# A two-layer graph network in fp32: one of seven products done in seven quarter products, and the output added in DRAM

## The chip, the cores and the metric

The kernel runs on one core of a Trainium2 chip. The time is device microseconds, the median of several runs; three runs of the kernel before gave 2488.0, 2488.44 and 2492.84 us. A profile of one more execution (2488.91 us) shows where the time lies. In tables PE is TensorE's matmuls, PEld its weight loads, DVE VectorE, ACT ScalarE, POOL GpSimd and SP SyncE.

## What is computed

128 graphs of 128 nodes with 512 features share one adjacency matrix. Two layers follow one another, each on a layer norm with a relu:

```python
# layer 0
h = relu(layernorm(x))
q, k, v = h @ Wq.T, h @ Wk.T, h @ Wv.T
rel = adj.T * (q @ k.T)
rel = rel / norm(rel, axis=2)
x = x + rel @ v
# layer 1
h = relu(layernorm(x))
q, k, v = h @ Wq + bq, h @ Wk + bk, h @ Wv + bv      # 8 heads of 64
scores = q @ k.T / 8 + where(adj == 0, -1e9, 0)
x = x + softmax(scores) @ v
```

All of it is fp32, inputs and output are x of 128x128x512.

## The kernel before

**Groups.** Four graphs make a group; there are 32 groups. In layer 0 the weights of Q and K are multiplied with each other once, so that layer 0 has two large products for each group (G and V) and layer 1 three (Q, K, V). Each is a product of 512x512 activations with 512x512 weights.

**Seven products for eight.** `Product` does each by the Winograd form of Strassen's method: both operands are cut into 2x2 quarters of 256x256, and seven products of quarters (`P1` to `P7`) and a few sums of quarters replace the eight. Each is four matmuls with a 128x128 stationary operand and a 128x256 moving one (`mm`, line 229). Sums of the weights' quarters are made once (`sums`), those of h for each group on VectorE (`sumA`, `sumB`). P1 and P2 together make the first quarter of the result: P1's result is kept in SBUF (`keep`), and VectorE adds P2's, out of PSUM, to it (`add`, line 253). For Q and K a bias is added on ScalarE while a result is kept (line 240); for layer 1's V it is on VectorE (line 246).

**Transposes by way of DRAM.** h, the softmax weights and the attention output are transposed by a store to scratch DRAM (`send_blocks`, on ScalarE's queue), a load back in blocks of 32 (`fetch_blocks`, on SyncE's queue, into two buffers `u` in turn), and a transpose of 32x32 blocks on VectorE: `hn`, `rd`, `T` for h; `ex`, `wr`, `wt` for the softmax weights; `oc`, `rdo`, `ot` for the output.

**The order.** All engines' queues follow one list of steps written by hand. Each engine takes its own instructions in the list's order. `FIRST`, `SECOND` and `LAST` are for the ends, `ORDER` runs for 30 of the 32 periods. In a period `m` is layer 0 of one group, `l` layer 1 of the group before it, `p` the end of the one before that, `f` the loading and statistics of the next, and `n` is `m`'s own layer 1 coming up. TensorE's part of `ORDER`, from the middle on, is layer 1's V (V.P1, P2, P5, P6, P3, P7), the scores `S3`, the first half of the attention `A0`, V.P4, and then with the next period Q.P1, Q.P2, K.P1, K.P2, Q.P5, Q.P6, Q.P3 and so on.

**The names that matter here.** `stat` makes a graph's mean and variance on VectorE, `inv` turns them into scale and shift on GpSimd, `hn` applies them on ScalarE. `mk3` masks the scores of graph 3, `exC2` and `exD2` are the two halves of graph 2's exponentials, `wr2` and `wt2` bring its transposed weights. `ot` (line 643) ends a pair of graphs: VectorE transposes (line 649) and scales by the softmax sums (line 654), GpSimd adds the result to x in SBUF (line 661) and stores it (line 662). x stays in one of 12 buffers from its load to that store.

**PSUM.** Eight banks: four in turn for products (`mm`), two for one graph's scores, two in turn (`po`) for `R`, `O`, `A` and half-score tiles.

Of the kernel before, what the change touches and what calls it, by code (L numbers as in the profile page):

```python
# [21 lines left out]
def kernel(  # L22
# [15 lines left out]
    nc = tc.nc  # L38
# [6 lines left out]
    HF = D // 2  # L45
    PSUM = bass.MemoryType.PSUM

    const = ctx.enter_context(tc.tile_pool(name="const", bufs=1))
    xpool = ctx.enter_context(tc.tile_pool(name="xpool", bufs=12))
    hpool = ctx.enter_context(tc.tile_pool(name="hpool", bufs=1))  # L50
    ppool = ctx.enter_context(tc.tile_pool(name="ppool", bufs=1))
    rpool = ctx.enter_context(tc.tile_pool(name="rpool", bufs=4))
# [42 lines left out]
    raw = {}
    for name, w, tag in (("q", wq0, "pq"), ("k", wk0, "pk"), ("v", wv0, "pv0")):
# [20 lines left out]
    def weights0(between):  # L117

        a12 = rpool.tile([P, 2, HF], F32, tag="r", name="a12")

        idle = ps_o.tile([P, P], F32, tag="po", name="idle")
        for _ in range(16):
            nc.tensor.transpose(idle, ident, ident)
        pa = [ps_mm.tile([P, D], F32, tag="mm", name=f"pa_{m}") for m in range(KD)]
        for k in range(KD):
            for m in range(KD):
                nc.tensor.matmul(
                    pa[m], lhsT=raw["q"][:, k, ts(m, P)], rhs=raw["k"][:, k, :],
                    start=(k == 0), stop=(k == KD - 1),
                )  # L130
# [30 lines left out]
    class Weights1:  # L161
# [7 lines left out]
        def sumw(self):  # L169
            sums("v0", w12["v0"], nc.gpsimd)  # L170

        def loadx(self):
            for b in range(G):
                load(2, b, nc.gpsimd)

        def sumq(self):
            sums("q", w12["q"], nc.vector)

# [27 lines left out]
    class Product:  # L206
# [65 lines left out]

        def P4(self):
            self.copy(self.quarter(1, 0), self.mm("x", T4N, self.h.x22, False), 0)

    class Layer:
        n: int
# [92 lines left out]
        def sumB(self):  # L370
            nc.vector.tensor_tensor(self.s[3], self.x12, self.s[1], ALU.subtract)
            nc.vector.tensor_tensor(self.s[2], self.x11, self.x21, ALU.subtract)

        def turned(self, k, b):
            return self.half[b // 2][:, k, ts(b % 2, P)]

    class Layer0(Layer):
        n = 0

        def start(self):  # L380
            g = self.g
            self.gT = ppool.tile([P, KD, G * P], F32, tag="pgv", name=f"gT_{g}")
            self.v = ppool.tile([P, G, D], F32, tag="pv0", name=f"v0_{g}")
            self.po = {}
            self.G = Product(self, "a", self.gT, True, name=f"pg_{g}")
            self.V = Product(self, "v0", self.v, False, name=f"pv0_{g}")
# [54 lines left out]
    class Layer1(Layer):  # L441
        n = 1

        def start(self):
            g = self.g
            self.qT = ppool.tile([P, NH, G * P], F32, tag="pq", name=f"qT_{g}")
            self.kT = ppool.tile([P, NH, G * P], F32, tag="pk", name=f"kT_{g}")
            self.Q = Product(self, "q", self.qT, True, bq_sb, name=f"pq_{g}")
            self.K = Product(self, "k", self.kT, True, bk_sb, name=f"pk_{g}")
            self.rs, self.wT, self.ps, self.nmax, self.po, self.e = {}, {}, {}, {}, {}, {}  # L450
            self.half_s = {}
            self.dw, self.uw, self.total, self.do, self.uo = {}, {}, {}, {}, {}
# [190 lines left out]
        def ot(self, i):  # L643
            g, u = self.g, self.uo.pop(i)
            for n in range(2):
                b = 2 * i + n
                xb = x_tiles.pop((g, b))
                o = work.tile([P, NH, TB, BK], F32, tag="o", name=f"o_{g}_{b}")
                nc.vector.transpose(
                    o.rearrange("p k t q -> p t k q"),  # L650
                    u[:, n * TB : (n + 1) * TB].rearrange("p t (k q) -> p t k q", q=BK),
                )
                heads = o.rearrange("p k t q -> p k (t q)").rearrange("p k (r d) -> p k r d", r=2)
                nc.vector.tensor_tensor(  # L654
                    heads, heads,
                    self.rs.pop(b).rearrange("p (r k) -> p k r", r=2)[:, :, :, None].to_broadcast(
                        [P, NH, 2, HD]
                    ),
                    ALU.mult,
                )  # L660
                nc.gpsimd.tensor_tensor(xb, xb, o.rearrange("p k t q -> p (k t q)"), ALU.add)  # L661
                nc.gpsimd.dma_start(out[g * G + b], xb)

    FIRST = """
        m.sumA m.sumB m.start f.stat0 f.stat1 f.inv0 m.G.P1 m.G.P2 f.stat2 f.stat3 f.inv1 w.sumw m.G.P5 f.hn0 f.rd0 m.G.P6
        w.scale m.G.P3 m.V.P1 f.hn1 f.rd1 w.sumv w.loadx m.G.P7 m.V.P2 w.sumq m.G.P4 m.V.P5
        m.R m.mask_rel m.square f.T0 m.V.P6 m.V.P3 m.N m.norms m.V.P7 m.O0 m.xO0 m.O1 m.xO1 n.stat0 n.stat1  # L670
        n.inv0 m.V.P4 n.hn0 n.rd0 f.T1 f.start f.G.P1 f.sumA m.O2 m.xO2 m.O3 m.xO3 n.stat2 n.stat3 n.inv1
        f.G.P5 f.sumB f.G.P6 n.hn1 n.rd1 f.G.P3 f.G.P7 n.T0 f.G.P2 f.G.P4 w.sumk n.T1 n.start
    """.split()
    SECOND = """
        l.Q.P1 l.sumA l.Q.P2 l.sumB l.K.P1 l.K.P2 l.Q.P5 l.Q.P6 f.load0 f.load1 l.Q.P3 l.K.P5 l.K.P6 l.Q.P7
        l.K.P3 l.K.P7 l.S0 l.mk0 f.load2 f.load3 l.Q.P4 l.K.P4 l.ex0 l.wr0 m.V.P1 f.stat0 f.stat1 f.inv0
        m.V.P2 m.V.P5 m.R m.mask_rel m.square f.stat2 f.stat3 f.inv1 m.V.P6 l.S1 m.N l.S2 l.mkA1 m.norms l.exC1
        l.mkB1 l.exD1 l.wr1 l.wt0 m.V.P3 l.add_mask2 m.V.P7 m.O0 m.xO0 m.O1 m.xO1 n.stat0 n.stat1 n.inv0
        m.V.P4 l.mx2 n.hn0 n.rd0 l.exC2 l.exD2 l.wr2 l.start_v l.V.P1 m.O2 m.xO2 m.O3 m.xO3 n.stat2 n.stat3 n.inv1
        l.V.P2 l.wt1 l.V.P5 n.hn1 n.rd1 l.V.P6  # L680
        l.V.P3 n.T0 l.V.P7 l.S3 l.A0 l.mk3 l.oc0 l.wt2 l.V.P4 l.ex3 n.T1 n.start
    """.split()
    ORDER = """
        l.Q.P1 p.rdo0 l.sumA l.Q.P2 p.wr3 m.hn0 l.sumB l.K.P1 m.rd0 l.K.P2 p.ot0 l.Q.P5 l.Q.P6 m.hn1 m.rd1
        l.Q.P3 l.Q.P7 p.wt3 m.T0 l.K.P5 l.K.P6 l.Q.P4 f.load0 f.load1 l.K.P3
        l.K.P7 m.T1 m.sumA m.sumB m.start m.G.P1 l.K.P4 m.G.P2 l.S0 p.A1 l.mk0 p.oc1 p.rdo1 m.G.P5 m.G.P6
        l.ex0 l.wr0 m.G.P3 m.V.P1 m.G.P7 p.ot1 m.V.P2 f.stat0 f.stat1 f.inv0 m.G.P4 m.V.P5
        l.wt0 f.load2 f.load3 m.R m.mask_rel m.square m.V.P6 l.S1 m.N l.S2 l.mkA1 m.norms l.exC1 l.mkB1 l.exD1
        l.wr1 m.V.P3 l.add_mask2 m.V.P7 m.O0 m.xO0 m.O1 m.xO1 n.stat0 n.stat1 n.inv0 m.V.P4 l.mx2
        n.hn0 n.rd0 l.exC2 l.exD2 l.wr2 l.start_v l.V.P1 m.O2 m.xO2 m.O3 m.xO3 n.stat2 n.stat3 n.inv1  # L690
        l.V.P2 l.wt1 l.V.P5 n.hn1 n.rd1 l.V.P6 f.stat2 f.stat3 f.inv1
        l.V.P3 n.T0 l.V.P7 l.S3 l.A0 l.mk3 l.oc0 l.wt2 l.V.P4 l.ex3 n.T1 n.start
    """.split()
# [21 lines left out]
    with tc.manual_schedule(engines={EN.PE, EN.SP, EN.Pool, EN.DVE, EN.Activation}):  # L715
        p, l, m = None, None, Layer0(0)
# [9 lines left out]
        f = Layer0(1)  # L726
# [40 lines left out]
```

## Time and profile before

| What | Value |
|---|---|
| median of three runs | 2488.44 us (2488.0 to 2492.84) |
| profiled execution | 2488.91 us, span 2487.1 us |
| TensorE busy, granted clock | 2479.4 us (100%), 1.000 |
| VectorE, ScalarE, GpSimd busy | 1724.2 us (69%), 1027.0 us (41%), 531.0 us (21%) |
| one period of `ORDER` | 76.55 us |
| data moved by DMA | 405.72 MB, mean 163 GB/s |
| x loads and output stores | 124 DMAs of 256 KB each on GpSimd's queue, median 3.1 and 3.0 us from issue to landing |

The profile gives for each engine its busy time, and for groups of equal instructions the mean time of one. The chain of waits follows the work back from the last instruction, at each step to what released it. A timeline lists one engine's instructions with start, length, and in brackets the idle time before and what ended it.

### The profile page before, as it was taken

The numbers are of one execution on the slowest core, as the hardware profiler recorded it, in microseconds if no ns is written. First come the engines' busy times: TensorE is split into PE (matmuls) and PEld (weight loads), VectorE is DVE, ScalarE is ACT, GpSimd is POOL, SyncE is SP. The second block draws the span as 40 slices with busy tenths as digits, with TensorE's granted clock in tenths as the row PEclk, the third lists the DMA queues.
The fourth block names the chain that finished last, engine by engine and source line by source line (L and its number), as shares of the span: only waits on it lengthen the run. The fifth ranks groups of instructions, "written<-read, shape, count | busy, mean of one in ns | idle before, by whom it ended". The sixth has DMA issues, their size and how long they took to land.

```text
span 2487.1 us, 40880 instructions
## 1 busy us (share of the span) xinstructions
PE 2479.4 (100%) x14688; PEld 2114.3 (85%) x14688; DVE 1724.2 (69%) x2549; ACT 1027.0 (41%) x3248; POOL 531.0 (21%) x944
## 2 busy tenths in 40 slices
PE   9999999999999999999999999999999999999999
PEld 7888888888888888888888888888888888888888
DVE  5666776667766677766677666776667776667766
ACT  3344443444433444434444344443344443343434
POOL 5111222122212212122122211221211212212111
PEclk9999999999999999999999999999999999999999
DMA  6256554565644556445555455554455644555544
GB/s 202 81 164 178 178 163 150 156 180 166 186 145 147 179 169 193 145 146 168 178 178 162 150 155 182 166 180 148 147 174 173 189 144 145 176 175 181 153 131 141
DMA packets 370619, 405.72 MB, mean 163 GB/s; under 512 B 29616, under 2 KB 287024, under 8 KB 370416
## 3 DMA queue, kind: packets, MB, share of 16 engines
q1 hardware_dynamic: 279520, 168.71, 26.4%
q10 hardware_dynamic: 70000, 165.96, 18.4%
q0 software_dynamic: 20896, 68.44, 8.4%
q8 instruction: 116, 1.90, 0.3%
q14 instruction: 87, 0.71, 0.1%
HBM read 204.80 MB, written 198.18 MB: 162 GB/s over the span
## 4 chain that ended last, share of the span: by engine, by line
PE 94%; DMA 2%; DVE 2%; issue 1%; SPq 1%; ACT 0%; POOL 0%; ACTq 0%; DVEq 0%; POOLq 0%
PE pv_x L229 16%; PE pg_x L229 9%; PE pq_x L229 8%; PE pk_x L229 8%; PE pv_z L229 8%; PE pg_z L229 5%; PE pr L393 5%; PE pq_z L229 5%; PE po L626 4%; PE pk_z L229 4%; PE pv_y L229 4%; PE po L433 4%; PE pss L471 4%; PE pg_y L229 2%; PE pq_y L229 2%; PE pk_y L229 2%
## 5 line engine op out<-in xcount | busy, mean ns | idle before, releaser
L661 POOL TENSOR_TENSOR xb<-xb,o 128x512 f32<-128x512 f32 x124 | 158.0, 1274 | 1175.2 <-DVE o L654 1157.4
L229 PE MATMUL pv_x<-wc_v,h 128*128 128x256 f32 x1280 | 300.8, 382 | 0.7 <-DVE pv_r L246 0.7
L229 PEld LDWEIGHTS pv_x<-wc_v,h 128*128 128x128 f32 x1280 | 240.4, 190 | 51.6 <-issue 20.0
L229 PE MATMUL pv_z<-wc_v,s 128*128 128x256 f32 x1024 | 245.1, 382 | 0.0
L324 DVE STREAM_TRANSPOSE h<-u_h 128x1024 f32<-128x1024 f32 x126 | 156.5, 1242 | 113.6 <-DMA u_h<-d_h 112.0
L312 ACT ACTIVATE hn<-xb,shift,rstd 128x512 f32<-128x512 f32 x252 | 191.0, 807 | 74.4 <-POOL shift L304 57.2
L229 PEld LDWEIGHTS pv_z<-wc_v,s 128*128 128x128 f32 x1024 | 191.9, 190 | 28.7
L495 ACT ACTIVATE e<-pss,nmax 128x128 f32<-128x128 f32 x504 | 177.7, 384 | 38.9 <-DVE nmax L488 38.9
L229 PE MATMUL pv_x<-wc_v,s 128*128 128x256 f32 x768 | 181.7, 379 | 0.0
L229 PE MATMUL pq_x<-h,wc_q 128*128 128x256 f32 x768 | 181.5, 379 | 0.0
L229 PE MATMUL pk_x<-h,wc_k 128*128 128x256 f32 x768 | 181.5, 379 | 0.0
L637 ACT COPY oT<-po 128x512 f32<-128x512 f32 x124 | 72.7, 586 | 259.6 <-PE po L626 196.2
L294 DVE BATCH_NORM_STATS2 st<-xb 128x6 f32<-128x512 f32 x256 | 171.9, 672 | 8.7 <-DMA xb<-in_x_dram 8.7
L229 PEld LDWEIGHTS pq_x<-h,wc_q 128*128 128x128 f32 x768 | 145.8, 190 | 19.9
L229 PEld LDWEIGHTS pk_x<-h,wc_k 128*128 128x128 f32 x768 | 145.8, 190 | 19.9
L510 DVE STREAM_TRANSPOSE wT<-u_w 128x1024 f32<-128x1024 f32 x126 | 152.8, 1213 | 9.4 <-DMA u_w<-d_w 8.1
L229 PEld LDWEIGHTS pv_x<-wc_v,s 128*128 128x128 f32 x768 | 143.3, 190 | 18.4 <-issue 0.2
L301 POOL TENSOR_SCALAR rstd<-mv 128x2 f32<-128x2 f32 x128 | 28.4, 222 | 478.1 <-DVE mv L295 475.7
L654 DVE TENSOR_TENSOR o<-o,rs 128x512 f32<-128x512 f32 x124 | 124.3, 1003 | 4.3
L229 PE MATMUL pg_z<-s,wc_a 128*128 128x256 f32 x512 | 124.1, 385 | 0.0
L229 PE MATMUL pq_z<-s,wc_q 128*128 128x256 f32 x512 | 121.8, 381 | 1.4 <-DVE qT L253 1.2
L626 PE MATMUL po<-wT,v 128*64 128x128 f32 x1984 | 122.0, 276 | 0.0
(157 smaller groups left out, 4839.0 us busy)
## 6 DMA issues: line engine op xcount, KB each, us to landing
d_h<-hn ACTq DMA_DIRECT2D x126, 512.0 KB, 4.2
u_h<-d_h SPq DMA_DIRECT2D x504, 128.0 KB, 3.8
d_w<-e ACTq DMA_DIRECT2D x126, 512.0 KB, 3.0
u_w<-d_w SPq DMA_DIRECT2D x504, 128.0 KB, 3.3
xb<-in_x_dram POOLq DMA_DIRECT2D x124, 256.0 KB, 3.1
d_o<-oT ACTq DMA_DIRECT2D x62, 512.0 KB, 3.7
u_o<-d_o SPq DMA_DIRECT2D x248, 128.0 KB, 3.2
out_dram<-xb POOLq DMA_DIRECT2D x124, 256.0 KB, 3.0
```

The costliest lines, as they stand in the source:

```text
L229: nc.tensor.matmul(ps[:, m, :], lhsT=lhsT, rhs=rhs, start=first and m == 0 and k == 0, stop=k == 1, skip_group_check=True,)
L294: nc.vector.bn_stats(st, x_tiles[g, b])
L312: nc.scalar.activation(hn[:, r], x_tiles[g, b].rearrange("p (k j q) -> p j k q", j=TB, q=BK), AF.Relu, bias=self.shift[:, b : b + 1], scal ...
L324: nc.vector.transpose(half.rearrange("p k (t i) -> p t k i", i=BK), self.u.pop(i).rearrange("p t (k q) -> p t k q", q=BK),)
L393: nc.tensor.matmul(pr[:, b, :], lhsT=self.turned(k, b), rhs=self.gT[:, k, ts(b, P)], start=(k == 0), stop=(k == KD - 1),)
L433: nc.tensor.matmul(po, lhsT=self.rel[:, b, :], rhs=self.v[:, b, :], start=True, stop=True)
L471: nc.tensor.matmul(half[r][:, k, :], lhsT=self.qT[rows, k, ts(b, P)], rhs=self.kT[rows, k, ts(b, P)], start=True, stop=True,)
L495: nc.scalar.activation(e[:, :, i, :], sc[:, i, :].rearrange("p (j q) -> p j q", q=BK), AF.Exp, bias=nmax[:, i : i + 1], accum_out=self.tot ...
L510: nc.vector.transpose(self.wT[b].rearrange("p h (t i) -> p t h i", i=BK), self.uw.pop(b).rearrange("p t (h q) -> p t h q", q=BK),)
L626: nc.tensor.matmul(po[r * HD : (r + 1) * HD, k, :], lhsT=self.v[:, b, ts(2 * k + r, HD)], rhs=wT[:, r * NH + k, :], start=True, stop=True,)
L654: nc.vector.tensor_tensor(heads, heads, self.rs.pop(b).rearrange("p (r k) -> p k r", r=2)[:, :, :, None].to_broadcast([P, NH, 2, HD]), ALU ...
L661: nc.gpsimd.tensor_tensor(xb, xb, o.rearrange("p k t q -> p (k t q)"), ALU.add)
```

## The change

P2 of Q and of layer 1's V is done, in the periods that run `ORDER`, by the same method once more: its operands are cut into 2x2 pieces of 128x128, and seven products of pieces, each one matmul of 128x128x128, replace the eight that four 128x256 matmuls hold. All seven go into one PSUM bank, `i`, in four slots that are used again; what the method adds up in a slot stays there and is accumulated. Between them results leave the slots by ScalarE copies and VectorE adds. The first quarter's missing addend, P1's result, is added at the end by GpSimd. The sums of pieces of the weights are made once on GpSimd (`sums2`), those of h for each group, also on GpSimd (`sumX`).

Layer 1's x is stored to the output in DRAM on SyncE's queue (`sto`) once its layer norm has read it; later the attention output is added to it there by a DMA that accumulates, on GpSimd's queue. GpSimd's add in SBUF goes away, and x has 8 buffers for 12. The loads of the third group move from the first period to the second. In the list the two halves of graph 2's exponentials move behind V.P2a and V.P2b, `wr2` with them, the statistics `f.stat2` and `f.stat3` behind V.P2c, and in `LAST` V.P6 moves ahead of graph 2's maxima.

```diff
-    xpool = ctx.enter_context(tc.tile_pool(name="xpool", bufs=12))
+    xpool = ctx.enter_context(tc.tile_pool(name="xpool", bufs=8))
...
+    def sums2(n: str, eng):
+        w, t = wc[n][:, W21], wi[n]
+        w11, w12_, w21, w22 = w[:, 0, 0:P], w[:, 0, P:HF], w[:, 1, 0:P], w[:, 1, P:HF]
+        eng.tensor_tensor(t[:, 0], w12_, w11, ALU.subtract)
+        eng.tensor_tensor(t[:, 1], w22, t[:, 0], ALU.subtract)
+        eng.tensor_tensor(t[:, 2], w22, w12_, ALU.subtract)
+        eng.tensor_tensor(t[:, 3], w21, t[:, 1], ALU.subtract)
...
-        def loadx(self):
-            for b in range(G):
-                load(2, b, nc.gpsimd)
...
+        def mi(self, slot: int, w, x, first=False):
+            if first:
+                pool, tag = (ps_o, "po") if self.turned else (ps_mm, "mm")
+                self.ps["i"] = pool.tile([P, 4, P], F32, tag=tag, name=f"{self.name}_i")
+            lhsT, rhs = (w, x) if self.turned else (x, w)
+            nc.tensor.matmul(
+                self.ps["i"][:, slot, :], lhsT=lhsT, rhs=rhs, start=first, stop=True, skip_group_check=True
+            )
...
+        def plus(self, i, j, slot):
+            nc.vector.tensor_tensor(self.block(i, j), self.ps["i"][:, slot, :], self.block(i, j), ALU.add)
+
+        def P2a(self):
+            self.mi(0, self.wq(0, 0), self.xq(0, 0), True)
+            self.mi(1, self.wq(1, 0), self.xq(0, 1))
+            self.mi(2, self.i[:, 0], self.h.sx[:, 0])
+            nc.scalar.copy(self.block(0, 0), self.ps["i"][:, 0, :])
+            nc.scalar.copy(self.block(1, 1), self.ps["i"][:, 2, :])
+
+        def P2e(self):
+            self.plus(0, 0, 1)
+
+        def P2b(self):
+            self.mi(0, self.i[:, 1], self.h.sx[:, 1])
+            self.mi(2, self.wq(1, 1), self.h.sx[:, 3])
+            nc.scalar.copy(self.block(0, 1), self.ps["i"][:, 0, :])
+
+        def P2f(self):
+            self.plus(0, 1, 2)
+
+        def P2c(self):
+            self.mi(0, self.i[:, 2], self.h.sx[:, 2])
+            self.plus(1, 1, 0)
+
+        def P2d(self):
+            self.mi(0, self.i[:, 3], self.xq(1, 1))
+            nc.scalar.copy(self.block(1, 0), self.ps["i"][:, 0, :])
+            nc.gpsimd.tensor_tensor(self.quarter(0, 0), self.quarter(0, 0), self.r.pop("r1"), ALU.add)
...
+        def sumX(self):
+            x = self.x12
+            x11, x12, x21, x22 = x[:, 0, 0:P], x[:, 1, 0:P], x[:, 0, P:HF], x[:, 1, P:HF]
+            self.sx = hpool.tile([P, 4, P], F32, tag=f"sx{self.n}", name=f"sx{self.n}_{self.g}")
+            nc.gpsimd.tensor_tensor(self.sx[:, 0], x21, x22, ALU.add)
+            nc.gpsimd.tensor_tensor(self.sx[:, 1], self.sx[:, 0], x11, ALU.subtract)
+            nc.gpsimd.tensor_tensor(self.sx[:, 3], x12, self.sx[:, 1], ALU.subtract)
+            nc.gpsimd.tensor_tensor(self.sx[:, 2], x11, x21, ALU.subtract)
...
+        def sto(self, i):
+            for b in range(2 * i, 2 * i + 2):
+                nc.sync.dma_start(out[self.g * G + b], x_tiles.pop((self.g, b)))
...
-                nc.gpsimd.tensor_tensor(xb, xb, o.rearrange("p k t q -> p (k t q)"), ALU.add)
-                nc.gpsimd.dma_start(out[g * G + b], xb)
+                nc.gpsimd.dma_start(out[g * G + b], o.rearrange("p k t q -> p (k t q)"), accum_op=ALU.add)
...
     ORDER = """
-        l.Q.P1 p.rdo0 l.sumA l.Q.P2 p.wr3 m.hn0 l.sumB l.K.P1 m.rd0 l.K.P2 p.ot0 l.Q.P5 l.Q.P6 m.hn1 m.rd1
-        l.Q.P3 l.Q.P7 p.wt3 m.T0 l.K.P5 l.K.P6 l.Q.P4 f.load0 f.load1 l.K.P3
+        l.Q.P1 l.Q.P2a p.rdo0 l.sumA p.wr3 m.hn0 l.sumB l.K.P1 m.rd0 l.K.P2 l.Q.P2e l.Q.P2b l.Q.P2f p.ot0 l.Q.P5
+        l.Q.P2c l.Q.P6 l.Q.P2d m.hn1 m.rd1
+        l.sto0 l.sto1 l.Q.P3 l.Q.P7 p.wt3 m.T0 l.K.P5 l.K.P6 l.Q.P4 f.load0 f.load1 l.K.P3
...
-        n.hn0 n.rd0 l.exC2 l.exD2 l.wr2 l.start_v l.V.P1 m.O2 m.xO2 m.O3 m.xO3 n.stat2 n.stat3 n.inv1
-        l.V.P2 l.wt1 l.V.P5 n.hn1 n.rd1 l.V.P6 f.stat2 f.stat3 f.inv1
-        l.V.P3 n.T0 l.V.P7 l.S3 l.A0 l.mk3 l.oc0 l.wt2 l.V.P4 l.ex3 n.T1 n.start
+        n.hn0 n.rd0 l.start_v l.V.P1 m.O2 m.xO2 m.O3 m.xO3 l.V.P2a l.exC2 n.stat2 n.stat3 n.inv1
+        l.V.P5 l.V.P2e l.V.P2b l.exD2 l.wr2 l.wt1 l.V.P2f l.V.P6 n.hn1 n.rd1 l.V.P2c f.stat2 f.stat3 f.inv1
+        l.V.P3 l.V.P2d n.T0 n.sumX l.V.P7 l.S3 l.A0 l.mk3 l.oc0 l.wt2 l.V.P4 l.ex3 n.T1 n.start
```

More of the change, by code (lines that the diff above doesn't have):

```diff
@@ L93, in sums @@
         eng.tensor_tensor(c[:, T4N], c[:, W21], c[:, T2], ALU.subtract)
+    wi = {n: const.tile([P, 4, P], F32, tag=f"wi_{n}", name=f"wi_{n}") for n in ("q", "v1")}
+    def sums2(n: str, eng):
[5 more added lines that the diff above has]
+        eng.tensor_tensor(t[:, 3], w21, t[:, 1], ALU.subtract)
     raw = {}
@@ L183, in sumv, with inner @@
             sums("v1", w12["v1"], nc.gpsimd)
+        def inner(self):
+            sums2("q", nc.gpsimd)
+            sums2("v1", nc.gpsimd)
     EN = mybir.EngineType
@@ L214, in __init__ @@
             self.bias, self.name, self.ps, self.r = bias, name, {}, {}
+            self.i = wi.get(n)
         def quarter(self, i, j):
@@ L274, in P4, with block, xq, wq @@
             self.copy(self.quarter(1, 0), self.mm("x", T4N, self.h.x22, False), 0)
+        def block(self, i, j):
+            if self.turned:
+                return self.dest[:, j, i * P : (i + 1) * P]
+            return self.dest[:, i, j * P : (j + 1) * P]
+        def mi(self, slot: int, w, x, first=False):
[6 more added lines that the diff above has]
+            )
+        def xq(self, i, k):
+            return self.h.x12[:, k, i * P : (i + 1) * P]
+        def wq(self, k, j):
+            return self.c[:, W21, k, j * P : (j + 1) * P]
+        def plus(self, i, j, slot):
[21 more added lines that the diff above has]
+            nc.gpsimd.tensor_tensor(self.quarter(0, 0), self.quarter(0, 0), self.r.pop("r1"), ALU.add)
     class Layer:
@@ L646, in ot @@
                 b = 2 * i + n
-                xb = x_tiles.pop((g, b))
                 o = work.tile([P, NH, TB, BK], F32, tag="o", name=f"o_{g}_{b}")
@@ L660, in ot @@
                 )
-                nc.gpsimd.tensor_tensor(xb, xb, o.rearrange("p k t q -> p (k t q)"), ALU.add)
-                nc.gpsimd.dma_start(out[g * G + b], xb)
+                nc.gpsimd.dma_start(out[g * G + b], o.rearrange("p k t q -> p (k t q)"), accum_op=ALU.add)
     FIRST = """
         m.sumA m.sumB m.start f.stat0 f.stat1 f.inv0 m.G.P1 m.G.P2 f.stat2 f.stat3 f.inv1 w.sumw m.G.P5 f.hn0 f.rd0 m.G.P6
-        w.scale m.G.P3 m.V.P1 f.hn1 f.rd1 w.sumv w.loadx m.G.P7 m.V.P2 w.sumq m.G.P4 m.V.P5
+        w.scale m.G.P3 m.V.P1 f.hn1 f.rd1 w.sumv m.G.P7 m.V.P2 w.sumq m.G.P4 m.V.P5
         m.R m.mask_rel m.square f.T0 m.V.P6 m.V.P3 m.N m.norms m.V.P7 m.O0 m.xO0 m.O1 m.xO1 n.stat0 n.stat1
@@ L674 @@
     SECOND = """
-        l.Q.P1 l.sumA l.Q.P2 l.sumB l.K.P1 l.K.P2 l.Q.P5 l.Q.P6 f.load0 f.load1 l.Q.P3 l.K.P5 l.K.P6 l.Q.P7
+        l.Q.P1 l.sumA l.Q.P2 l.sumB w.inner l.K.P1 l.K.P2 l.Q.P5 l.Q.P6 l.sto0 l.sto1 f.load0 f.load1 l.Q.P3 l.K.P5 l.K.P6 l.Q.P7
         l.K.P3 l.K.P7 l.S0 l.mk0 f.load2 f.load3 l.Q.P4 l.K.P4 l.ex0 l.wr0 m.V.P1 f.stat0 f.stat1 f.inv0
@@ L680 @@
         l.V.P2 l.wt1 l.V.P5 n.hn1 n.rd1 l.V.P6
-        l.V.P3 n.T0 l.V.P7 l.S3 l.A0 l.mk3 l.oc0 l.wt2 l.V.P4 l.ex3 n.T1 n.start
+        l.V.P3 n.T0 n.sumX l.V.P7 l.S3 l.A0 l.mk3 l.oc0 l.wt2 l.V.P4 l.ex3 n.T1 n.start
     """.split()
     ORDER = """
-        l.Q.P1 p.rdo0 l.sumA l.Q.P2 p.wr3 m.hn0 l.sumB l.K.P1 m.rd0 l.K.P2 p.ot0 l.Q.P5 l.Q.P6 m.hn1 m.rd1
-        l.Q.P3 l.Q.P7 p.wt3 m.T0 l.K.P5 l.K.P6 l.Q.P4 f.load0 f.load1 l.K.P3
+        l.Q.P1 l.Q.P2a p.rdo0 l.sumA p.wr3 m.hn0 l.sumB l.K.P1 m.rd0 l.K.P2 l.Q.P2e l.Q.P2b l.Q.P2f p.ot0 l.Q.P5
+        l.Q.P2c l.Q.P6 l.Q.P2d m.hn1 m.rd1
+        l.sto0 l.sto1 l.Q.P3 l.Q.P7 p.wt3 m.T0 l.K.P5 l.K.P6 l.Q.P4 f.load0 f.load1 l.K.P3
         l.K.P7 m.T1 m.sumA m.sumB m.start m.G.P1 l.K.P4 m.G.P2 l.S0 p.A1 l.mk0 p.oc1 p.rdo1 m.G.P5 m.G.P6
@@ L689 @@
         l.wr1 m.V.P3 l.add_mask2 m.V.P7 m.O0 m.xO0 m.O1 m.xO1 n.stat0 n.stat1 n.inv0 m.V.P4 l.mx2
-        n.hn0 n.rd0 l.exC2 l.exD2 l.wr2 l.start_v l.V.P1 m.O2 m.xO2 m.O3 m.xO3 n.stat2 n.stat3 n.inv1
-        l.V.P2 l.wt1 l.V.P5 n.hn1 n.rd1 l.V.P6 f.stat2 f.stat3 f.inv1
-        l.V.P3 n.T0 l.V.P7 l.S3 l.A0 l.mk3 l.oc0 l.wt2 l.V.P4 l.ex3 n.T1 n.start
+        n.hn0 n.rd0 l.start_v l.V.P1 m.O2 m.xO2 m.O3 m.xO3 l.V.P2a l.exC2 n.stat2 n.stat3 n.inv1
+        l.V.P5 l.V.P2e l.V.P2b l.exD2 l.wr2 l.wt1 l.V.P2f l.V.P6 n.hn1 n.rd1 l.V.P2c f.stat2 f.stat3 f.inv1
+        l.V.P3 l.V.P2d n.T0 n.sumX l.V.P7 l.S3 l.A0 l.mk3 l.oc0 l.wt2 l.V.P4 l.ex3 n.T1 n.start
     """.split()
@@ L696 @@
         p.A1 p.oc1 p.rdo1 l.K.P3 l.Q.P7 l.S0 l.mk0 l.K.P7 l.ex0 l.wr0 l.Q.P4 p.ot1 l.K.P4 l.S1 l.mkA1 l.exC1
-        l.start_v l.V.P1 l.mkB1 l.exD1 l.wr1 l.V.P2 l.wt0 l.V.P5 l.S2 l.S3 l.add_mask2 l.mx2 l.exA2 l.exB2 l.V.P6
+        l.start_v l.V.P1 l.mkB1 l.exD1 l.wr1 l.V.P2 l.wt0 l.V.P5 l.S2 l.S3 l.add_mask2 l.V.P6 l.mx2 l.exA2 l.exB2
         l.mkA3 l.exA3 l.V.P3 l.V.P7 l.tw2 l.wt1 l.mkB3 l.exB3 l.V.P4 l.An0 l.fin0 l.An1 l.fin1 l.tw3 l.An2 l.fin2
```

## The prediction

> **What bounds the kernel now.** I read the page's first parts, then the chain of waits over one period, then the timelines of VectorE, ScalarE and GpSimd in a period.
>
> ```profile
> span 2487.1 us, 40880 instructions
> PE 2479.4 (100%) x14688; PEld 2114.3 (85%) x14688; DVE 1724.2 (69%) x2549; ACT 1027.0 (41%) x3248; POOL 531.0 (21%) x944
> PEclk9999999999999999999999999999999999999999
> PE 94%; DMA 2%; DVE 2%; issue 1%; SPq 1%; ACT 0%; POOL 0%; ACTq 0%; DVEq 0%; POOLq 0%
> ```
>
> TensorE is busy all of the span at its full granted clock. A microsecond of its work that goes is a microsecond won, and a microsecond that it waits is one lost. The busy table of one period, from one layer-1 Q's first product to the next, says the same:
>
> ```profile
> 1202.78:1279.33 76.55, 76.55 (x458) 65.53 (x457) 53.89 (x80) 31.90 (x103) 16.15 (x29) 1.00 0.53 164
> ```
>
> 76.55 us, all of it TensorE. Now the chain of waits, whose lines give start, length and count (weight loads and matmuls together):
>
> ```profile
> 1245.68 1.73 PE pv_z L229 x8
> 1247.41 3.57 PE pr L393 x32
> 1274.42 1.09 PE pss L471 x16
> 1275.51 1.90 PE po L626 x32
> 1277.41 1.93 PE pv_x L229 x8
> ```
>
> A product of four 128x256 matmuls takes 1.73 us, 0.432 each. The 16 matmuls of 128x128 of `R` take 3.57 us, 0.223 each, with their weight loads hidden. A product after `A` takes 1.93: when a full weight load can't go ahead, 0.19 us of it is exposed.
>
> VectorE, in the part where the change acts (start, length, what it waited for in brackets):
>
> ```profile
> 1268.01 0.18 DVE L295 BATCH_NORM_AGGREGATE mv<-st 128x2 f32<-128x6 f32 x1
> 1268.10 0.66 DVE L253 TENSOR_TENSOR v<-pv_y,pv_r 128x512 f32<-128x512 f32 x1
> 1271.00 0.69 DVE L246 TENSOR_TENSOR pv_r<-pv_x,bv_sb 128x512 f32<-128x512 f32 x1 [0.45 <-PE pv_x L229]
> ...
> 1282.13 1.25 DVE L324 STREAM_TRANSPOSE h<-u_h 128x1024 f32<-128x1024 f32 x1 [1.20 <-DMA u_h<-d_h]
> 1285.94 0.69 DVE L372 TENSOR_TENSOR h<-h,h 128x512 f32<-128x512 f32 x1
> 1286.54 0.69 DVE L253 TENSOR_TENSOR kT<-pk_y,pk_r 128x512 f32<-128x512 f32 x1
> 1288.89 0.71 DVE L649 STREAM_TRANSPOSE o<-u_o 128x512 f32<-128x512 f32 x1 [1.66 <-DMA u_o<-d_o]
> 1290.98 1.31 DVE L654 TENSOR_TENSOR o<-o,rs 128x512 f32<-128x512 f32 x1
> ```
>
> VectorE is only 69% busy, but here it runs late: `K.P2`'s add ran at 1286.54, though TensorE had left `K.P2` at 1286.08, because the second transpose of h (`T1`) had waited for its transfer. Today nothing on TensorE needs these results soon.
>
> ```profile
> 1270.16 1.52 ACT L312 ACTIVATE hn<-xb,shift,rstd 128x512 f32<-128x512 f32 x2 [0.48 <-DVE wT L510]
> 1271.71 0.38 ACTq L195 DMA_DIRECT2D d_h<-hn  x1
> ```
>
> ```profile
> 1273.39 0.22 POOL L301 TENSOR_SCALAR rstd<-mv 128x2 f32<-128x2 f32 x1 [3.54 <-DVE mv L295]
> 1274.78 0.20 POOL L304 TENSOR_TENSOR shift<-shift,rstd 128x2 f32<-128x2 f32 x1
> 1290.47 1.27 POOL L661 TENSOR_TENSOR xb<-xb,o 128x512 f32<-128x512 f32 x1 [15.49 <-DVE o L654]
> ```
>
> From the `d_h` issue (1271.71) to `T1` (1282.13) it is 10.42 us by way of DRAM. A group of four small GpSimd steps (`inv`) takes 1.59, one 128x512 add there 1.27.
>
> **What the change gives.** 30 of the 32 periods (those run from `ORDER`) do P2 of Q and of layer 1's V in seven 128x128 matmuls: 7 x 0.223 = 1.56 us for 1.73, so 0.17 a product, 0.33 a period, 9.9 us in all. Half of a 128x256 matmul (0.216) and 0.223 bound the matmul from both sides; I take the row of `R`. First, second and last periods keep the old P2.
>
> **What it adds to TensorE's path: waits.** The seven products share one PSUM bank. In the built program the first matmul of `P2b` waits until VectorE's `P2e` add has read that bank, `P2c`'s waits for `P2f`, `P2d`'s for the add of `P2c`. TensorE takes its queue in order, so all later products stand behind. I follow the period from V's P2 (start 1265.62 on TensorE's timeline), moving all by these waits. Sizes that no row has: a 128x128 VectorE add lies on the line through 0.42 (128x256) and 0.69 (128x512), so 0.29; a 128x128 ScalarE copy from PSUM follows its predecessor after about 0.3 (the 128x256 ones come 0.37 apart).
>
> 1. `V.P2b`. P2a 0.67, so `V.P5` runs 1266.29 to 1268.02. Ahead of `P2e`, VectorE must add the bias to P5's result, which waits for P5: start 1268.22 (the 0.20 by which the row at 1271.00 follows TensorE's 1270.80), 0.61 to the next instruction, 0.29 for `P2e`: 1269.12. With 0.19 of weight load: **1.29 us**. P2b then ends at 1269.76. No VectorE backlog can be blamed: stats end at 1268.1 as before.
> 2. `A0` needs v's first quarter, whose last addend is now a GpSimd add behind `f.inv1`. P6 ends at 1271.49; bias add to 1272.30, P2c's add 1272.59, two pairs of stats 1.61 to 1274.20, inv 0.09+1.59 to 1275.88, add 0.1+1.27 to 1277.25. TensorE is done with `S3` at 1276.48: **0.8 us**. A0 ends near 1279.2.
> 3. `Q.P2b`. ScalarE's exp of block 2 is split by the new copies: copy to 1270.26, four exps 1.38, d_w issue 0.45, `hn1` 1.52, so d_h goes out at 1273.65 and, 10.42 later, `T1` starts at 1284.07. T1 and four sums take 3.81 (1282.13 to 1286.54 less the P2 add between, 0.60): 1287.88. K.P2's add 0.61, `P2e` 0.29: 1288.78. TensorE has finished K.P2 at 1286.89 (1279.2 + 1.83 + 1.73 + 0.67 + 3.46). With the weight load: **2.1 us**.
> 4. `Q.P2d` waits for P2c's add, which VectorE holds behind `p.ot0`. Its data came 11.55 after A0's end in this period (10.96 in the middle one of all): 1290.2 to 1290.75; four operations 2.70, add 0.29: about 1293.4 with P2f ahead. TensorE: 1288.97 + 0.45 + 1.73 + 0.22 + 1.73 = 1293.10. With the load, **0.5 us**.
>
> P2c in both products is ready in time: V.P2f ends near 1270.6, P6 at 1271.49; Q.P2f near 1290.3, Q.P5 at 1291.15. Sum of the waits 4.7; less 0.33 it is +4.4 us a period, times 30 = **+132**. On the profiled execution (2488.91: its span and 1.8 around it; 0.5 above the median 2488.44) that is 2621; I say 2620.
>
> **What is costed at nothing, and its cover.** ScalarE gains 8 copies (2.4 us of a period's 44.7 idle); their lateness is in step 3. GpSimd loses four adds (5.1 us) and gains two (2.5) and four 128x128 ones (0.2 to 1.27 each by its smallest and its 128x512 row; 0.46 by the line, 1.85 together); these `sumX` steps start at 1277.3 and Q.P2a's third matmul comes at 1283.2, covered by A0, V.P4, Q.P1; without cover up to 1.9. The Q quarter's GpSimd add (near 1294) is wanted by S0, ten products later. SP gets four stores behind `m.rd1`, ahead of `p.rdo1` by some 10 us; xb's loads wait for them on GpSimd's queue (stores about 3 us), the stats that use xb come near 1323: covered, at worst 3 us late without reaching TensorE. `wr2` goes out about 1.9 us later, so `wt2` may start near 1281 for 1279.1; T1 behind it on VectorE waits till 1284 anyway. Eight small GpSimd sums of weights, the loads of group 2 moved to the second period, and V.P6's place in `LAST` happen once: at most a few us of other engines, none on TensorE. Ahead of these loads and behind them stand the accumulating DMAs, the issue at 0.58 each as the plain ones had. The accumulating writes come on top of the stores, 124 x 0.262 = 32.5 MB, and a read of the same again if accumulation reads its target: 8 to 16% on 405.72 MB, with DMA at 0.53. Each 0.3 us of lateness of u_h would add 0.3 to step 3: 0 to +30 us, I take 0; a gain is not excluded but has no source here.
>
> **Two rules of the Trainium skill.** The PEclk row is full everywhere, with no gaps to test it. "TensorE: Matmul & The Clock Gate", "Part 1: The HAM clock gate", says that an idle window of about 3.4 us halves the clock until the array has again been busy as long. That speaks against a change that adds waits: one trip a period would cost an estimated 1.7 us, +51 in all. My gaps are at most 2.1, so I count none. For GpSimd's adds the rows of `L654` are 0.69 alone and 1.31 beside `L661` (1.27 either way). "SBUF — State Buffer", "SBUF: two separate sides", calls the shared port an exclusive lock, where the later one blocks for the whole instruction. By the rows VectorE wins 2 x 0.62 a period and GpSimd's new adds keep 1.27; by the rule the V add could lose up to 0.69 behind a VectorE add of two SBUF inputs (+21 us). At that place VectorE runs transposes, PSUM adds and mask steps, so I keep the row.
>
> **The rivals.** (A) *Only the built-in waits bind*: T1 and ot0 arrive early enough, GpSimd in time. The two P2b waits alone are 1.29 + 1.29 (0.20, 0.61, 0.29, 0.19 behind K.P2), less 0.33: +67, 2556. For it: step 3 rests on a chain through DRAM. Against: T1 waits for u_h in the trace. 12%. (B) *Transfers get slower*, or the clock trips: +30 to +51, 2650 to 2672. 17%. (C), the other side: *the bank waits are met before TensorE comes*, as they would be if VectorE ran `P2e` ahead of P5's and K.P2's adds; then only step 4's remnant could stay, and the time is 2479. It decides when P2e ends within 1.7 us of P2a. Against it: P2e's place on VectorE's queue behind an add that waits for the very product TensorE has just left. 5%. That the quarter products aren't made can't be: the built program has seven 128x128 matmuls there. My forecast has 65%, and 1% is left for no change.
>
> **How the numbers follow.** 2620 is the likeliest case; 2550 takes in A, 2670 most of B. 0.2% (5 us) is about what a measurement can tell from no change. Slower 0.94, same 0.01, faster 0.05.
>
> **What would show it.** Idle TensorE ahead of `pv_i` and `pq_i` with VectorE adds as releaser, 1.3 and 2.1 us long, 30 times each; ahead of `po` with GpSimd's v add; a period of 81 us. A period under 76.3 would make me wrong; a Q wait of 1.3 would mean A.

## The result and the profile after

Four runs of the changed kernel gave a median of 2606.17 us (2603.08 to 2607.65), beside 2488.62 (2488.0 to 2492.84) for the kernel before: +117.6 us, a ratio of 1.0468 [1.0456, 1.0480]. It is slower, by some 4 us in each of the 30 periods that were changed.

The page's first parts for the changed kernel (its profiled execution took 2605.76 us):

```profile
span 2603.9 us, 42063 instructions
PE 2495.2 (96%) x15048; PEld 2113.5 (81%) x15048; DVE 1697.1 (65%) x2669; ACT 1078.3 (41%) x3488; POOL 550.8 (21%) x1012
PEclk9999999999999999999999999999999999999999
PE 75%; DMA 9%; ACT 6%; DVE 5%; issue 2%; SPq 1%; ACTq 1%; POOL 1%; DVEq 0%; POOLq 0%
```

The span grew by 117 us. TensorE's busy time grew by only 16, and its share fell from all of the span to 96%. So nearly all the new time is TensorE waiting. The last line says the same in another way: the chain that ended last was 94% TensorE and is now 75%, the rest runs through DMA, ScalarE and VectorE. Busy shares of the other engines hardly moved; none of them became the bound. A stretch of one period's length (bounds, length, then busy time of PE, PEld, DVE, ACT and POOL, granted clock, DMA share, GB/s):

```profile
604.48:684.65 80.17, 77.06 (x470) 65.42 (x469) 52.70 (x84) 33.60 (x111) 16.73 (x31) 1.00 0.62 172
```

80.17 us for 76.55, with 3.1 us in it when no matmul ran. TensorE's list of waits names who ended them (total us, times, longest). The changed kernel, then the kernel before:

```profile
PE pq_i L300 <- DVE qT L311: 55.1, 39, 2.7
PE pv_i L300 <- DVE v L311: 29.4, 30, 1.0
PE po L705 <- POOL v L338: 14.7, 29, 0.5
```

```profile
PE pq_z L229 <- DVE qT L253: 1.2, 2, 0.9
PE pv_x L229 <- DVE pv_r L246: 0.7, 1, 0.7
```

In the kernel before, all waits on VectorE's `qT` came to 1.2 us and those on V's results to 0.7. Now the first two rows are matmuls of the quarter products (line 300) waiting for VectorE's adds (`plus`, line 311), and the third is `A0` waiting for the GpSimd add (line 338) that gives v its last addend. 99 us stand in these three rows. The same three places on TensorE's timeline in one period (start, length, idle time before and what ended it):

```profile
600.91 0.49 PE L300 MATMUL pv_i<-wi_v,sx 128*128 128x128 f32 x2 [0.98 <-DVE v L311]
...
608.84 1.97 PE L705 MATMUL po<-wT,v 128*64 128x128 f32 x32 [0.50 <-POOL v L338]
...
616.69 1.89 PE L241 MATMUL pk_y<-h,wc_k 128*128 128x256 f32 x8
620.21 0.46 PE L300 MATMUL pq_i<-sx,wi_q 128*128 128x128 f32 x2 [1.62 <-DVE qT L311]
```

And VectorE around the last of them:

```profile
614.43 1.25 DVE L388 STREAM_TRANSPOSE h<-u_h 128x1024 f32<-128x1024 f32 x1 [0.60 <-DMA u_h<-d_h]
...
617.77 0.68 DVE L436 TENSOR_TENSOR h<-h,h 128x512 f32<-128x512 f32 x1
619.17 0.69 DVE L265 TENSOR_TENSOR kT<-pk_y,pk_r 128x512 f32<-128x512 f32 x1 [0.71 <-ACT pk_r L252]
619.78 0.28 DVE L311 TENSOR_TENSOR qT<-pq_i,qT 128x128 f32<-128x128 f32 x1
```

`P2e` is the last row: 0.28 us of work, on data that TensorE had made by 615. It ran at 619.78 because it stands behind `K.P2`'s add, and TensorE waited for it until 620.21. `K.P2`'s add itself waited 0.71 us for ScalarE's `pk_r`.

### The profile page after: what moved, and what is told of

Its sections match the earlier page's. It is cut to its first block, busy times and chain, and to the rows that moved or that the text cites. A ratio compares the mean times of both kernels' runs of the same rounds, so it can differ in the third digit from the quotient of the medians.

```text
span 2603.9 us, 42063 instructions
## 1 busy us (share of the span) xinstructions
PE 2495.2 (96%) x15048; PEld 2113.5 (81%) x15048; DVE 1697.1 (65%) x2669; ACT 1078.3 (41%) x3488; POOL 550.8 (21%) x1012
## 3 DMA queue, kind: packets, MB, share of 16 engines
HBM read 204.80 MB, written 230.69 MB: 167 GB/s over the span
## 4 chain that ended last, share of the span: by engine, by line
PE 75%; DMA 9%; ACT 6%; DVE 5%; issue 2%; SPq 1%; ACTq 1%; POOL 1%; DVEq 0%; POOLq 0%
PE pv_x L241 11%; PE pg_x L241 8%; PE pv_z L241 7%; PE pk_x L241 7%; PE pq_x L241 6%; PE pg_z L241 4%; PE pr L467 4%; PE pk_z L241 4%; PE po L507 4%; PE pq_z L241 4%; DMA u_h<-d_h 3%; PE po L705 3%; PE pss L550 3%; ACT e L574 2%; PE pg_y L241 2%
## 5 line engine op out<-in xcount | busy, mean ns | idle before, releaser
L739 POOL DMA_DIRECT2D out_dram<-o x124 | 111.9, 902 | 969.9 <-DVE o L732 955.8
L70 POOL DMA_DIRECT2D xb<-in_x_dram x124 | 73.7, 597 | 334.2 <-DMA out_dram<-xb 310.6
L705 PEld LDWEIGHTS po<-wT,v 128*64 128x64 f32 x1984 | 107.0, 137 | 24.4 <-POOL v L338 20.2
```

The lines of the kernel that those rows point to most:

```text
L705: nc.tensor.matmul(po[r * HD : (r + 1) * HD, k, :], lhsT=self.v[:, b, ts(2 * k + r, HD)], rhs=wT[:, r * NH + k, :], start=True, stop=True,)
L739: nc.gpsimd.dma_start(out[g * G + b], o.rearrange("p k t q -> p (k t q)"), accum_op=ALU.add)
```

## The experiments

All edits but one move steps in the lists or give a slot its own bank; the work is the changed kernel's. Each was run beside the kernel before on the same chip, whose median was 2488.3 to 2488.6 in all of them.

**V's wait alone.** `V.P2e` goes ahead of the bias add that waits for P5.

```diff
-        ... n.stat2 n.stat3 n.inv1
-        l.V.P5 l.V.P2e l.V.P2b ...
+        ... n.stat2 l.V.P2e n.stat3 n.inv1
+        l.V.P5 l.V.P2b ...
```

> Only V's P2e add is put earlier on VectorE, between the statistics of graphs 2 and 3, ahead of the bias add of V.P5. Theory (TensorE waits for VectorE readers of the shared PSUM bank): the wait ahead of V.P2b, 0.98 us plus exposed weight load, 1.24 us a period in the changed kernel, goes, but P2f then decides for V.P2c (VectorE holds it behind the weights' transpose): about 0.3 comes back. Net 0.9 to 1.2 us a period over 30 periods: 2570 to 2579. Rival (the loss is slower transfers or the quarter matmuls themselves): 2606, no change.

Measured: 2582.16 us (2577.59 to 2582.79), 1.0370 [1.0353, 1.0387]; 24.0 less than the changed kernel. The wait at `V.P2b` is gone from the list, and A0's fell to 4.8 us in all. The total ahead of Q's quarter matmuls rose to 62.5. The time stayed above what was expected, and the trace shows why: TensorE's clock. Two views of this kernel: the timeline around one long wait, and the busy table of a 20 us stretch around another (clock third from the end).

```profile
214.73 1.89 PE L241 MATMUL pk_y<-h,wc_k 128*128 128x256 f32 x8
219.87 0.46 PE L300 MATMUL pq_i<-sx,wi_q 128*128 128x128 f32 x2 [3.25 <-DVE qT L311]
...
220.38 3.42 PE L241 MATMUL pq_z<-s,wc_q 128*128 128x256 f32 x8
```

```profile
1240.00:1260.00 20.00, 17.44 (x113) 14.74 (x112) 14.06 (x20) 8.59 (x29) 5.26 (x9) 0.91 0.83 224
```

Behind the wait, Q.P5 (`pq_z`) takes 3.42 us where the same product takes 1.89, and 0.91 over 20 us is 1.8 us of clock lost. Summed over the stretches below full clock (one at the very end left out), 13.6 us were lost in this profiled execution, after seven waits, beside 3.4 in that of the changed kernel, after two. Without the 13.6 its 2582.77 would be 2569, just under what was expected.

**Q's wait, moved and then removed.** First only `Q.P2e` goes ahead, behind `sumA`, long before K.P2's add:

```diff
-        ... l.sumA p.wr3 m.hn0 ... l.K.P2 l.Q.P2e l.Q.P2b ...
+        ... l.sumA l.Q.P2e p.wr3 m.hn0 ... l.K.P2 l.Q.P2b ...
```

> Only Q's P2e add is put earlier, behind the first two sums of h. Theory: the 1.86 us ahead of Q.P2b go, and most of it comes back ahead of Q.P2d, since the add of P2c still stands behind the transposes and scalings of p.ot0: wait there 0.2 grows to about 1.4. Net -0.65 us a period: about 2587. Rival (transfers, matmuls): 2606. If the Q wait could be won alone: 2550.

Measured: 2589.29 us (2585.58 to 2596.0), 1.0408 [1.0389, 1.0427]. This is near what was expected, and much less than the 55 us of waits. The list of waits still has 39.7 us ahead of Q's quarter matmuls, now at `P2d`:

```profile
618.33 0.49 PE L300 MATMUL pq_i<-h,wi_q 128*128 128x128 f32 x2 [0.82 <-DVE qT L311]
```

`P2c`'s add stands behind `ot0` on VectorE, and once TensorE comes earlier it meets this wait in full. So the second experiment also moves `ot0` behind it:

```diff
-        ... l.Q.P2f p.ot0 l.Q.P5
-        l.Q.P2c l.Q.P6 ...
+        ... l.Q.P2f l.Q.P5
+        l.Q.P2c p.ot0 l.Q.P6 ...
```

> As the one before, and p.ot0 is put behind Q.P2c's add. Theory: both Q waits go, 2.1 to 2.3 us a period: 2537 to 2543. Rival: 2606, or no better than the one before.

Measured: 2532.62 us (2531.35 to 2533.6), 1.0177 [1.0162, 1.0192], 73.6 less than the changed kernel and a little under what was expected. No wait ahead of `pq_i` is left in the list. Two waits stood in a row on one engine's path, and taking away the first alone paid only a fourth of what both paid.

**A second bank.** Here `Q.P2e` stays late, where the change put it; only `ot0` moves as above, and Q's slot 1, the one that `P2e` reads, lies in a bank of its own.

```diff
+            if self.turned and slot == 1:
+                bank = self.ps["i1"] = ps_o.tile(...)
+                first = True
...
+            bank = self.ps["i1" if self.turned and slot == 1 else "i"]
```

> The changed kernel with p.ot0 behind Q.P2c's add, and, in Q alone, the second of the first three small products in a bank of its own; P2e stays late, behind K.P2's add. Then no write of P2b goes to a bank that P2e has yet to read. Theory (the wait is for the bank's reader, not for data): Q's waits go with no step of P2 moved, as in the kernel with P2e early and p.ot0 late: 2530 to 2538, V's waits stay. Rival (VectorE's lateness there delays TensorE whatever the banks): 2580 or more.

Measured: 2535.63 us (2534.27 to 2536.33), 1.0193 [1.0178, 1.0209]. TensorE and VectorE in a period of it:

```profile
601.98 1.89 PE L241 MATMUL pk_y<-h,wc_k 128*128 128x256 f32 x8
603.70 0.39 PE L304 MATMUL pq_i<-sx,wi_q 128*128 128x128 f32 x2
```

```profile
604.43 0.69 DVE L265 TENSOR_TENSOR kT<-pk_y,pk_r 128x512 f32<-128x512 f32 x1 [1.01 <-ACT pk_r L252]
```

K.P2's add is as late as ever and `P2e` still behind it, yet `P2b` follows K.P2 without a gap. The matmul never needed `P2e`'s result; it needed the bank free of its reader. The Trainium skill ("PSUM — Partial Sum Buffer", "PSUM bank collisions raise a hardware error") says that engines are to be kept apart by bank and quadrant and not by address, which is what the built program does; no run here lets two engines meet on one bank, so only the price of the guard is shown. V was left with one bank, and its wait stayed at 29.4 us.

**What holds K.P2's add.** The prediction said `T1`, which waits for u_h from DRAM; the timeline above says ScalarE. With `ot0` moved as before, `m.hn0` (1.5 us on ScalarE) goes behind K.P1's results:

```diff
-        ... p.wr3 m.hn0 l.sumB l.K.P1 m.rd0 ...
+        ... p.wr3 l.sumB l.K.P1 m.hn0 m.rd0 ...
```

> The changed kernel with two moves in Q: p.ot0 behind Q.P2c's add, and m.hn0 behind the keeping of K.P1's result on ScalarE. It asks what held K.P2's add on VectorE, and with it Q.P2b, beyond the wait for K.P2 itself. If it is ScalarE's late K.P1 result (the trace of the changed kernel shows 0.71 us of waiting for it): idle time ahead of Q.P2b falls from 1.62 to about 1.07 us, a period from 80.2 to 79.4, about 2582. If it is the transpose T1 and the sums behind it (the prediction's step 3): idle stays at 1.6, 2598.

Measured: 2578.61 us (2575.52 to 2579.25), 1.0358 [1.0344, 1.0372]. That is near the time expected if ScalarE holds the add, and far from the other. The wait ahead of `Q.P2b` fell from 1.63 to 1.14 us in the median period, and VectorE's bracket now names the product itself:

```profile
616.30 0.69 DVE L265 TENSOR_TENSOR kT<-pk_y,pk_r 128x512 f32<-128x512 f32 x1 [0.38 <-PE pk_y L241]
```

The 1.1 us that remain are what the order alone costs: K.P2's add cannot start before TensorE has left K.P2, and `P2e` comes behind it.

**The output half alone.** The kernel before with the store of x on SyncE's queue, the accumulating DMA and 8 buffers, without any quarter product.

```diff
-                nc.gpsimd.tensor_tensor(xb, xb, o.rearrange("p k t q -> p (k t q)"), ALU.add)
-                nc.gpsimd.dma_start(out[g * G + b], xb)
+                nc.gpsimd.dma_start(out[g * G + b], o.rearrange("p k t q -> p (k t q)"), accum_op=ALU.add)
```

> The kernel before with the other half of the change alone: x stored on SyncE's queue, attention output added in DRAM, 8 buffers of x; no quarter products. Theory (all of the loss is TensorE's waits at the shared bank): 2488, within 5 us. Rival (the accumulating DMAs' traffic makes transposed tiles late): 2500 to 2570, with TensorE idle ahead of the products that use h.

Measured in 13 runs: 2489.66 us (2488.35 to 2492.53), 1.0004 [0.9996, 1.0012]. Its busy line:

```profile
PE 2477.9 (100%) x14688; PEld 2114.4 (85%) x14688; DVE 1686.8 (68%) x2549; ACT 1027.0 (41%) x3248; POOL 417.5 (17%) x820
```

GpSimd loses 113 us and VectorE 37, and the time does not move: neither was on the path. So the +117.6 comes with the quarter products. (These with the old add in SBUF were not run.)

**All the waits taken away.** To the moves of V and Q above this adds `V.P2f` ahead of the second half of graph 2's exponentials, and `f.inv1` behind `V.P2d`, so that GpSimd's v add need not stand behind it.

```diff
-        ... l.exD2 l.wr2 l.wt1 l.V.P2f l.V.P6 ... f.stat3 f.inv1
-        l.V.P3 l.V.P2d n.T0 ...
+        ... l.V.P2f l.exD2 l.wr2 l.wt1 l.V.P6 ... f.stat3
+        l.V.P3 l.V.P2d f.inv1 n.T0 ...
```

> All waits taken out by order alone: V's and Q's P2e early, P2f of V ahead of the weights' transpose, p.ot0 behind Q.P2c, f.inv1 behind GpSimd's add to v. Theory: only the saving of the quarter products is left, 0.33 us a period: 2478 to 2484, below the kernel before (2488.6). Rival (part of the loss is transfers or the quarter matmuls): stays over 2500.

Measured: 2502.37 us (2500.36 to 2503.27), 1.0054 [1.0039, 1.0069], not the 2478 to 2484 expected, and inside what the rival had given, over 2500. But the trace shows waits of the same kind: 13.7 us of waits stayed ahead of Q's quarter matmuls in 23 periods, because `P2e` now stands behind T1:

```profile
1287.44 1.25 DVE L388 STREAM_TRANSPOSE h<-u_h 128x1024 f32<-128x1024 f32 x1 [1.64 <-DMA u_h<-d_h]
...
1290.06 0.28 DVE L311 TENSOR_TENSOR qT<-pq_i,qT 128x128 f32<-128x128 f32 x1
```

With everything else early, the transfer that the prediction had blamed does bind. So the last order, the spread order, gives Q's bank more products in between: `Q.P5` ahead of `Q.P2b`, and `Q.P2d` behind `Q.P7`.

```diff
-        ... l.K.P2 l.Q.P2b l.Q.P2f l.Q.P5
-        l.Q.P2c p.ot0 l.Q.P6 l.Q.P2d m.hn1 m.rd1
-        l.sto0 l.sto1 l.Q.P3 l.Q.P7 p.wt3 ...
+        ... l.K.P2 l.Q.P5 l.Q.P2b l.Q.P2f p.ot0 l.Q.P6
+        l.Q.P2c m.hn1 m.rd1
+        l.sto0 l.sto1 l.Q.P3 l.Q.P7 l.Q.P2d p.wt3 ...
```

> Like the kernel with all waits taken out by order, but Q.P2b moves behind Q.P5 on TensorE, Q.P2d behind Q.P7, and p.ot0 back ahead of P2c's add, so that every reader of the bank has one product or more of time. That kernel's best periods were 76.29 us, its mean 77.03. Theory: all periods near 76.3, the saving of the quarter products shows: 2478 to 2484 and below the kernel before. Rival (the quarter products gain nothing, each small matmul costs what it saves): 2488 or more.

Measured in 20 runs: 2485.45 us (2481.57 to 2488.57), 0.9987 [0.9980, 0.9994]. It beats the kernel before by 3.2 us, though it stays a little above the 2484 expected at most. The rivals, by which part of the loss lies in transfers or in the quarter matmuls and no order removes it, are out. The median period is 76.26, 0.29 below the 76.55 of before. What is left in the list of waits:

```profile
PE pv_z L241 <- DVE pv_r L258: 2.5, 1, 2.5
PE pv_x L241 <- DVE v L265: 2.0, 3, 1.1
PE pq_z L241 <- DVE s L431: 1.4, 4, 0.6
...
PE pq_i L300 <- DVE qT L311: 0.4, 1, 0.4
```

The bank costs nothing any more. Of the 9 to 10 us that 30 shorter periods are worth, more than half is lost to scattered waits like these and to smaller gaps. The largest is in `LAST`, so the same kernel was run once more with the `LAST` of the kernel before:

```diff
-        ... l.add_mask2 l.V.P6 l.mx2 l.exA2 l.exB2
+        ... l.add_mask2 l.mx2 l.exA2 l.exB2 l.V.P6
```

> The spread order with LAST as in the kernel before (V.P6 behind graph 2's exponentials). The spread kernel's trace shows 2.5 us of TensorE idle ahead of one V.P3 in LAST, waiting for VectorE. Theory: that one wait is LAST's move, so 1 to 2.5 us go: 2483 to 2484.5. Rival (it is lateness carried from the period ahead): 2485.5, no change.

Measured in 13 runs: 2486.47 us (2484.83 to 2490.54), 0.9993 [0.9985, 1.0001]. No gain; a wait of 2.2 us in `LAST` stayed, so the move in `LAST` is not its cause. That leaves lateness carried in from the periods ahead; what it begins with stays open.

## Why the prediction held, and where it did not

It gave 2620 within 2550 to 2670; measured was 2606. The mechanism was the one named: seven quarter products in one bank, `P2e` behind an add that waits for the product TensorE has just left. The experiments that took that away, by order or by a second bank, took the time away with it. Its steps, by the median period (start to start, less the products' own time):

| Step | predicted | measured |
|---|---|---|
| saved by 7 x 0.223 for 1.73, two products | 0.33 | 0.29 to 0.33 (median and best period of the spread order, 76.26 and 76.22) |
| 1. `V.P2b` | 1.29 | 1.24 (0.98 idle, the rest an exposed weight load) |
| 2. `A0` | 0.8 | 0.58 |
| 3. `Q.P2b` | 2.1 | 1.86 |
| 4. `Q.P2d` | 0.5 | 0.18 (mean 0.31) |
| sum less the saving | 4.4 | 3.6 (median period 76.55 to 80.16) |

**Step 1 held.** It rested on VectorE's order alone: an add that follows TensorE by a known time, one 0.61, one 0.28.

**Steps 2 and 4 were sized too high**, by 0.2 and 0.3 us. Both were sums of four to seven small operations on another engine, less a TensorE time. They are small differences of large terms, and in 21 of the 30 periods no more than the weight load of some 0.2 us is left of step 4.

**Step 3 held in size by luck; its cause was wrong.** It put K.P2's add behind T1 and T1 behind 10.42 us from the `d_h` issue. Measured were 9.12 us, with u_h landing 3.0 us after its issue for 3.8 before. In the median period VectorE was done with T1 and the sums 0.1 us after TensorE left K.P2 (618.46 and 618.42 in the rows above). In the run with `hn0` moved K.P2's add starts 0.27 us after, with nothing else to wait for, so T1 cost nothing. The last holder was ScalarE's `pk_r`, ready 0.72 us after TensorE left K.P2. In the kernel before it was ready at 1285.87, ahead of TensorE's 1286.08. The kernel before, then the changed kernel:

```profile
1285.03 0.84 ACT L240 ACTIVATE pk_r<-pk_x,bk_sb 128x256 f32<-128x256 f32 x2 [0.45 <-ACT hn L312]
```

```profile
616.00 0.27 ACT L317 COPY qT<-pq_i 128x128 f32<-128x128 f32 x1
616.15 0.29 ACT L318 COPY qT<-pq_i 128x128 f32<-128x128 f32 x1
616.31 1.54 ACT L376 ACTIVATE hn<-xb,shift,rstd 128x512 f32<-128x512 f32 x2
...
618.30 0.84 ACT L252 ACTIVATE pk_r<-pk_x,bk_sb 128x256 f32<-128x256 f32 x2 [0.44 <-ACT hn L376]
```

The step gave ScalarE's work ahead of `pk_r` a price of nothing except through `d_h`. The two new copies hold it up by 0.3 us. The larger part is TensorE's own: only the three quarter matmuls of P2a (0.67 us) stand ahead of K.P1 where all of P2 (1.73) stood, so TensorE leaves K.P2 1.06 us sooner after Q.P1. Beyond the 1.29 that the order costs, the step had 0.8 us for T1; the runs show nothing there and 0.5 for ScalarE, the part that moving `hn0` took away. ScalarE is 41% busy; the share said nothing of this place.

**The sum.** The four steps are 0.8 us a period too high, 23 us over 30; against the +132, only 14.5 was missing, since the periods' mean (80.45 for 76.65) grew by 0.2 more than their median, 6 us, and the ends cost some 3.

**What was costed at nothing** held on the whole. `sumX` steps took 0.45 each (0.46 by the line), GpSimd's v add 1.27; the xb loads stood 310.6 us in all behind the stores on GpSimd's queue, and no engine on the path missed them. The DMA half took 32.6 MB more and, by itself, 1 us or none. **The shared port**: the scaling in `ot` takes 693 ns for 1003 before, and the v add kept 1.27. But this doesn't speak against the rule, whose price of up to 21 us was not put to the test: beside none of the 30 v adds did VectorE run an operation with both inputs in SBUF. In the kernel before the rows do what the rule says: each of the 62 scalings that met a GpSimd add had started behind it, and ended 0.55 us after it.

**The clock gate was not quite free**, and here the prediction's "I count none" failed. In the profiled execution two of the Q waits were followed by a stretch at half clock. One of them on the timeline, and the busy table of the 3.6 us behind it (granted clock third from the end):

```profile
1905.71 0.46 PE L300 MATMUL pq_i<-sx,wi_q 128*128 128x128 f32 x2 [1.88 <-DVE qT L311]
...
1906.37 3.43 PE L241 MATMUL pq_z<-s,wc_q 128*128 128x256 f32 x8
```

```profile
1905.80:1909.40 3.60, 3.60 (x12) 2.98 (x13) 2.06 (x4) 0.27 (x1) 0.06 (x1) 0.54 0.84 225
```

3.6 us at 0.54 is 1.7 us of clock lost, twice 3.4, at the price of one trip that the prediction had estimated, but in 2 of 30 periods. The page's PEclk row shows none of it: a tenth is too coarse and a slice of 65 us too long.

**The rivals.** A (2556, only the built-in waits): its two waits of 1.29 are what V measured and close to what moving `hn0` left to Q (1.14 idle and a weight load); A0, ScalarE and P2d made the rest. B, slower transfers: u_h landed sooner. C (2479, waits met before TensorE comes): not this kernel, but the spread order is its case, `P2e` run early, and came to 2485.

## What to carry to other kernels

Before splitting a product into many small ones in one PSUM bank, write down for each small matmul which engine reads the bank before it, and what stands ahead of that reader on its queue. An add ahead that waits for the product TensorE has just left makes a stall that no spare capacity covers; move the reader ahead of it, put another whole product in between, or give the reader a bank of its own. And after removing one wait look for the next in line before judging: here the first alone paid a fourth of the pair.

## What was not expected of the hardware

**Short waits can halve the clock.** Over the eleven traces, none of some 95 TensorE waits between 1.0 and 1.8 us was followed by a lower granted clock. Of 34 from 1.8 us up, 16 were, the shortest 1.87, while one of 2.73 was not. Each cost about 1.7 us, one of them twice that. "TensorE: Matmul & The Clock Gate", "Part 1: The HAM clock gate", of the Trainium skill speaks of an idle window of about 3.4 us, in windows that run freely; here less idle time than that was enough about every second time.

The traces' clock records show which waits count. The end of each trace left out, the stretches at half clock within one execution all begin on one grid with a step of 3.413 us, and last one step of it (one lasted two). In the changed kernel they begin at 1906.06 and 1987.98, 24 steps apart. The step ahead of the first and that step itself:

```profile
1902.65:1906.06 3.41, 1.53 (x9) 1.09 (x8) 2.84 (x6) 1.29 (x3) 0.00 (x0) 1.00 0.79 256
1906.06:1909.47 3.41, 3.41 (x11) 2.79 (x11) 2.13 (x4) 0.27 (x1) 0.13 (x1) 0.50 0.80 206
```

In the step ahead of each of the 16, TensorE was idle for 1.87 to 2.70 us. Of all other steps (the start and the end of each trace left out) three had 1.88 to 1.96 us, none more. So in these traces it took about 1.9 us of idle time within one step, and a wait that lies across two can be longer without harm: the one of 2.73 had 1.88 in one and 0.85 in the next. Such stretches may be part of the scatter of the run with `Q.P2e` alone moved (10 us over four runs; mean clock 0.997 to 0.999, the longer runs at the lower clocks, and 0.002 of 2590 us are 5), but only one execution of each kernel has a trace.

**The accumulating DMA.** Issuing it takes GpSimd 902 ns for the plain store's 580. The kernel before, then the changed one (busy us, mean ns, idle time ahead):

```profile
L662 POOL DMA_DIRECT2D out_dram<-xb x124 | 71.9, 580 | 39.4 <-POOL xb L661 36.5 <-issue 2.9
```

```profile
L739 POOL DMA_DIRECT2D out_dram<-o x124 | 111.9, 902 | 969.9 <-DVE o L732 955.8
```

It lands 4.9 us after its issue (median) for 3.0 of the plain one. HBM writes rose from 198.18 to 230.69 MB while reads stayed at 204.80: if the accumulation reads its target, that does not show in this counter, and whether it costs bandwidth stays open.
